# Two convolutional attention layers on one core: who evicts q and k, where zeros are written, and the order and queues of the last units

## The chip, the core and the metric

The kernel runs on one core of one Trainium2 chip. The metric is the device time of one execution in microseconds; the runs before the change have a median of 3063.85 us (three runs, 3060.79 to 3065.46). A core has five engines that run their own instruction queues and meet at semaphores: TensorE (PE in the profile) multiplies matrices into PSUM, VectorE (DVE) and ScalarE (ACT) work on SBUF and PSUM, GpSimd (POOL) and SyncE (SP) here mostly start DMAs. Sixteen DMA engines move data between DRAM and SBUF, whichever engine started the transfer.

## The reference

Two layers act on x, two images of 256 channels and 64 x 64 pixels, all in fp32. Layer 0 is attention over all 4096 pixels with 8 heads of 32 channels, mixed with x by a mask that is enlarged from 32 x 32:

```
q, k, v = conv1x1(x, Wq, bq)/sqrt(32), conv1x1(x, Wk, bk), conv1x1(x, Wv, bv)
fuse = softmax(q k^T) v                       # per head, 4096 x 4096
hybrid = conv1x1(concat(x, fuse), Wf, bf)
x = hybrid * m + x * (1 - m)
```

Layer 1 gates the channels, attends inside windows of 8 x 8 pixels, shuffles the channels and ends with two grouped 7 x 7 convolutions that give a gate:

```
x = x * sigmoid(relu(x @ ca_w1 + ca_b1) @ ca_w2 + ca_b2)
x = x + out_proj(window_attention(x))          # 4 heads of 64, windows of 64 tokens
x = channel_shuffle(x)
y = relu(bn1(conv7x7(x, sa_w1, groups=64)))
y = bn2(conv7x7(y, sa_w2, groups=64))
out = x * sigmoid(y)
```

## The kernel before

The order of the work on each engine is written out by hand; the framework adds only the waits. There are three parts.

**First part (L369 to L512).** x is cut into 16 chunks of 512 pixels (8 per image). For each chunk TensorE makes q and then k for 256 channels, 8 matmuls each (L432), into pairs of PSUM banks, of which three rotate. For each half `g` of the channels VectorE adds the bias and writes the result to SBUF (L442), and ScalarE squares the same PSUM half with the same bias into `sq` (L443). SyncE stores q (L447) and k (L450) to DRAM, and loads the chunk three ahead (L403). VectorE takes the largest sums of squares (L451), and one chunk later TensorE sums them by head (`norms`, L412): the product of the largest norms of q and k says whether the softmax can do without subtracting its maximum. The staging tiles of q, k and `sq` have two buffers each. After the 16 chunks TensorE makes v, 16 matmuls a chunk (L469); ScalarE copies it (L477) and GpSimd stores it (L482).

Beside this a generator `prepare` makes the constants, one step per chunk: GpSimd fetches weights and mask, VectorE folds the batch norms into the convolution weights. Its end writes zeros into the DRAM tensor `w_s` (16 units of 128 x 1792 floats, 896 KB each), from a zero tile in SBUF, by 16 DMAs of GpSimd (L327).

**Attention (L517 to L1182).** The 1024 `slots` are (image, chunk of 512 queries, half of the heads, block of 128 keys). In a slot TensorE makes the scores of four heads (L630), ScalarE their exponentials (L640), TensorE multiplies with v (L659) and VectorE adds the exponentials up (L661). k and v come in pieces of four slots, loaded two pieces ahead by SyncE into three buffers (L557, L559). Before the first slot SyncE issues, in this order, q, two pieces, the x chunk (L570) and the mask (L573); the third piece follows. After both halves of a chunk of queries, `stage` does the rest of layer 0 and the window attention in small steps between the slots (L718 to L979), and writes the rows to `x_s` in DRAM, on GpSimd (L976).

Between the slots another generator, `bands`, turns the convolution weights into band matrices: 156 DMAs of GpSimd within DRAM, which write strided elements into `w_s` over the zeros (L347, L353, L360). Every sixth slot takes one step of it (L1179). The steps stand in GpSimd's queue in that order, between the stores of the stages' rows, but a step waits for no slot.

**Last part.** `convolve` (L989) works through `items`, pairs of a unit (four groups of channels) and the images done together: units 0 to 6 of image 0, then units 1 to 6 of image 1, units 7 to 15 of both, at last unit 0 of image 1. For each item TensorE does the first convolution (L1040, from the rows loaded at L1019), ScalarE the relu (L1048), TensorE the second (L1064), ScalarE the tanh and a scaling (L1074, L1080), VectorE the product with x (L1086), and DMAs store the result, 12 per image, in turn by GpSimd and SyncE (L1096), for the last item by ScalarE and SyncE. The product tile z has two buffers. Weights of a unit come by SyncE (`load_w`, L1012) into the eight buffers that held exponentials, unit 0 into one of its own; unit u+8 is loaded when image 1's item of unit u is done.

The items are interleaved with the last stage, that of image 1's last rows: the stage gives `yield True` at six points (after L751, L791, L870, L877, L918, L945), and at each of them one step of `convolve` goes in. A step is either the second convolution of item k, or its product and stores and the first convolution of item k+2. Image 0 only is known then; rows with image 1 can be loaded once the stage has stored the last of them (`staged`). Loads of items 7 to 10 are then issued at once by `more()`, ahead of the next item's stores on SyncE.

```
items = [(u, (0,)) for u in range(EARLY)] + [(u, (1,)) for u in range(1, EARLY)]
items += [(u, (0, 1)) for u in range(EARLY, NU)] + [(0, (1,))]
```

Of the kernel before, what the change touches and what calls it, by code (L numbers as in the profile page):

```python
# [10 lines left out]
F32 = mybir.dt.float32  # L11
I32 = mybir.dt.int32
AF = mybir.ActivationFunctionType
# [4 lines left out]
B, C, H, W = 2, 256, 64, 64  # L18
N = H * W
P = 128  # L20
KC = C // P
# [9 lines left out]
EB = 8  # L31
DN = 8
EARLY = 7
# [13 lines left out]
NU = NG // UG  # L47
UW = UG * KS
# [7 lines left out]
def conv_seq_kernel(ctx: ExitStack, tc: tile.TileContext, a, out):  # L56
    nc = tc.nc
    const = ctx.enter_context(tc.tile_pool(name="const", bufs=1))
    dram = ctx.enter_context(tc.tile_pool(name="dram", bufs=1, space=bass.MemoryType.DRAM))
# [66 lines left out]
    w_s = dram.tile([NU, P, 2 * 32 * UW], F32, name="ws")  # L126
# [29 lines left out]
    for h in range(2):  # L156
        pending.append((cb1[64 * h : 64 * h + 64], a["ca_b1"]))
        pending.append((cw2[64 * h : 64 * h + 64], a["ca_w2"]))

    r1_s = dram.tile([32 + 4, NU, UW], F32, name="r1s")  # L160
    r2_s = dram.tile([32 + 4, NU, 4, UW // 4], F32, name="r2s")

# [2 lines left out]
    def prepare(mk, cwp):  # L165
# [55 lines left out]
        zero = cwp.tile([P, 2 * 32 * UW], F32, name="zero")  # L221
# [50 lines left out]
        for name, t in (  # L272
# [4 lines left out]
            g, beta, mean, var, cbias = (t[:, :, i] for i in range(5))  # L277
# [28 lines left out]
        for i in range(4):  # L306
            h, k = i % 2, i // 2
# [15 lines left out]
        nc.gpsimd.dma_start(  # L323
            r2_s.rearrange("p u i f -> p (u i f)"), m2.rearrange("p u i q x -> p (u i q x)")
        )
        for u in range(NU):
            nc.gpsimd.dma_start(w_s[u], zero)  # L327
            if u % 4 == 3:
                yield

# [5 lines left out]
    def bands():  # L338
        band1 = w_s.rearrange("u p (m f) -> u (p m) f", f=UW)
        band2 = w_s.rearrange("u p (m f) -> u (p m) f", f=UW // 4)  # L340
        for q in range(4):
            for dy in range(KS):
                r0, r1 = max(0, dy - PAD), min(RB, RB + dy - PAD)
                p0, m0, n = 32 * q + 1 + r0, 1 + r0 - dy + PAD, r1 - r0
                k = KS * q + dy
                at0, step = p0 * 64 + m0, 64 + 1
                nc.gpsimd.dma_start(  # L347
                    band1[:, at0 : at0 + step * (n - 1) + 1 : step, :], spread(r1_s[k : k + 1], n)
                )
                yield  # L350
                for i in range(4):
                    at0, step = p0 * 256 + 128 + i * 32 + m0, 256 + 1
                    nc.gpsimd.dma_start(  # L353
                        band2[:, at0 : at0 + step * (n - 1) + 1 : step, :],
                        spread(r2_s[k : k + 1, :, i], n),
                    )
                    yield
            for i in range(4):
                at0 = 32 * q * 256 + 128 + i * 32 + 1
                nc.gpsimd.dma_start(  # L360
                    band2[:, at0 : at0 + RB, :], spread(r2_s[32 + q : 33 + q, :, i], RB)
                )
                yield
# [5 lines left out]
    with (  # L369
# [8 lines left out]
        for n in ("WqT", "WkT", "WvT"):  # L378
            t = w0.tile([P, KC, C], F32, name=n)
# [3 lines left out]
        bias = {}  # L383
        for n in ("bq", "bk"):
            t = w0.tile([P, KC], F32, name=n)
# [33 lines left out]
        last = None  # L419
        for i, (b, c) in enumerate(chunks):  # L420
            load_chunk()
            x = xs0[i]
            sq = st0.tile([P, 2 * KC, CH], F32, tag="sq", name=f"sq_{b}_{c}")
            tops = st0.tile([P, 2 * KC, CH // 4], F32, tag="top4", name=f"top4_{b}_{c}")
            for n, w in (("q", wq), ("k", wk)):
                s = psum2(f"{n}0_{b}_{c}")
                for g in range(KC):
                    for kc in range(KC):
                        rhs = x[:, kc, :]
                        if n == "q":  # L430
                            rhs = rhs.rearrange("p (r w c) -> p w r c", r=WS, w=NW)
                        nc.tensor.matmul(  # L432
                            s[:, g, :],
                            w[:, kc, g * P : (g + 1) * P],
                            rhs,
                            start=(kc == 0),
                            stop=(kc == KC - 1),
                        )
                t = st0.tile([P, KC, CH], F32, tag=n, name=f"{n}st_{b}_{c}")
                bt = bias["b" + n]  # L440
                for g in range(KC):
                    nc.vector.tensor_scalar_add(t[:, g, :], s[:, g, :], bt[:, g : g + 1])  # L442
                    nc.scalar.activation(  # L443
                        sq[:, g + KC * (n == "k"), :], s[:, g, :], AF.Square, bias=bt[:, g : g + 1]
                    )
                if n == "q":
                    nc.sync.dma_start(q_s[b, c], t.rearrange("p g n -> p (g n)"))  # L447
                else:
                    for g in range(KC):
                        nc.sync.dma_start(k_s[b, g, c], t[:, g, :])  # L450
            nc.vector.tensor_reduce(  # L451
                tops, sq.rearrange("p g (n f) -> p g n f", f=4), AX.X, ALU.max
            )
            if i:
                norms(i - 1, last)
            last = tops
            for t, src in pending[4 * i : 4 * i + 4]:
                nc.scalar.dma_start(t, src)
            next(prepared, None)
# [61 lines left out]
    def pipeline(arm, shifted, pools):  # L521
# [196 lines left out]
        def stage(b, c):  # L718
# [173 lines left out]
                    )  # L892
            window_exp(1)
            nc.scalar.copy(v, sv)
            yield
            normalise(1)
            yield

# [83 lines left out]

        items = [(u, (0,)) for u in range(EARLY)] + [(u, (1,)) for u in range(1, EARLY)]
        items += [(u, (0, 1)) for u in range(EARLY, NU)] + [(0, (1,))]
        staged = []

        def convolve():  # L989
# [6 lines left out]
            for k in range(2):  # L996
                t = cpool.tile([P, B * nb, WP], F32, name=f"yc{arm}{k}")
                nc.gpsimd.memset(t, 0.0)
                ycs.append(t)
            xs, ws, ys = {}, {}, {}  # L1000
            dst = out.rearrange("b (g i) r w -> b i r g w", i=4)

            def load_w(u):
                if u >= NU:
                    return
                n = 2 * 32 * UW
                if u == 0:
                    t = cpool.tile([P, n], F32, name=f"w{arm}{u}")
                else:
                    t = ep.tile([P, HG, CH], F32, tag="e", name=f"w{arm}{u}")  # L1010
                    t = t.rearrange("p h n -> p (h n)")[:, 0:n]
                nc.sync.dma_start(t, w_s[u])  # L1012
                ws[u] = t
# [69 lines left out]
            def gate(k, z):  # L1083
                u, images = items[k]
                x = xs[k][:, 0 : nb * len(images), :, PAD : PAD + W]
                nc.vector.tensor_mul(z, z, x.rearrange("p n g x -> p g n x"))  # L1086

                last = k == len(items) - 1
                engines = (nc.scalar, nc.sync) if last else (nc.gpsimd, nc.sync)
                stores = 0  # L1090
                for m, b in enumerate(images):
                    for n, (x0, r0, r1) in enumerate(BLOCKS):
                        for i in range(4):
                            p = 32 * i + 1 - x0
                            stores += 1
                            engines[stores % len(engines)].dma_start(  # L1096
                                dst[b, i, r0:r1, UG * u : UG * u + UG, :],
                                z[p + r0 : p + r1, :, nb * m + n, :],
                            )
# [21 lines left out]
            for k, (u, images) in enumerate(items):  # L1121
                while len(xs) <= k + 1 < len(items):
                    if not more():
                        yield
                conv1(k + 1)
                yield
                more()
                z = conv2(k)
                yield
                more()  # L1130
                gate(k, z)
                if xcs or k + 4 < EARLY:
                    load_rows(k + 4)
                if B - 1 in images and u:
                    load_w(u + EB)

        def run_later():
            for _ in range(len(later)):
# [22 lines left out]
        for i, (b, c, g, m) in enumerate(slots):  # L1161
            now[0] = i
            if (b, c, g, m) == (B - 1, NCHUNK - 1, 0, 0):
                conv = convolve()
                next(conv)
            if m % PB == 0:
                load_piece(i // PB + AHEAD)
            if g == KC - 1 and m == 0:
                nxt = (b, c + 1) if c + 1 < NCHUNK else (b + 1, 0)
                if nxt[0] < B:  # L1170
                    load_q(*nxt)
            rest = scores(i + 2) if i + 2 < len(slots) else None
            products(i)
            if rest:
                rest()
            if g == KC - 1 and m == NMB - 1:
                at(DN + 5, lambda b=b, c=c: stages.append(stage(b, c)))
            run_later()
            if i % 6 == 1:  # L1179
                next(banded, None)  # L1180
            if i % 4 == 0:
                run_stages()  # L1182
# [102 lines left out]
```

## Time and profile before

The profiled execution took 3056.05 us; its span, from the first to the last instruction, is 3054.1 us. The granted TensorE clock is 0.99 of full speed on the mean.

| part of the span | us | TensorE busy | VectorE busy | ScalarE busy | DMA share |
|---|---|---|---|---|---|
| first part, to the first scores | 0 to 218.1 | 189.7 | 96.0 | 63.0 | 0.69 |
| attention | 218.1 to 2816.0 | 2574.6 | 2399.4 | 2303.6 | 0.31 |
| last part | 2816.0 to 3054.1 | 209.2 | 47.7 | 82.5 | 0.51 |

Busy times are sums of an engine's instructions; the DMA share is the mean busy share of the sixteen DMA engines. A busy TensorE is not TensorE at its peak, as matmuls overlap and their ends are modelled. In a row of the timeline, the bracket at the end says how long the engine was idle before the instruction, and what it then waited for. That releaser is inferred from semaphores: the last one to come by the profile.

In the first part VectorE spends 64 x 0.75 us at L442 and 16 x 2.29 us at L451, ScalarE 64 x 0.69 us at L443. The sixteen stores of zeros are issued from 103.1 to 129.4 us and take 23.2 us each (median) to land. In the last part a one-image item takes TensorE 2.5 us for the first and 3.6 us for the second convolution, a two-image item 4.8 and 5.0 us. A store of the result takes GpSimd 0.57 us of its queue.

### The profile page before, as it was taken

What the parts mean: (1) busy time and instruction counts of PE and PEld (TensorE: products, weight loads), DVE (VectorE), ACT (ScalarE), POOL (GpSimd) and SP (SyncE); (2) the same over time, 40 slices, a digit from 0 to 9 for tenths busy, and PEclk for the clock granted to TensorE, in tenths of its full rate; (3) what the DMA queues carried; (4) which work ended last, traced back from release to release, by engine and by line L of the source; (5) the groups of instructions that cost most, each with busy time, mean ns of one, the idle gap of its engine ahead of it and who ended that gap; (6) DMA issues with size and microseconds to landing.
All of it is one profiled execution on the core that took longest, in us unless ns stands there. A gap on an engine that the chain in (4) does not pass through costs nothing.

```text
span 3054.1 us, 60829 instructions
## 1 busy us (share of the span) xinstructions
PE 2973.5 (97%) x25114; PEld 1007.6 (33%) x25114; DVE 2543.1 (83%) x1411; ACT 2449.0 (80%) x4115; POOL 358.5 (12%) x617
## 2 busy tenths in 40 slices
PE   8899989999999999999999999999999999999997
PEld 3372222232322222222222222222222222233675
DVE  5519989999999999898999998999999998999111
ACT  2239979898989899898989898989898998988333
POOL 8130000001010101010100001010101010000256
PEclk9999999999999999999999999999999999999998
DMA  7854212324242424242322324232424242413364
GB/s 214 322 176 79 63 51 63 68 60 73 62 77 60 67 73 73 66 67 74 62 72 60 66 60 73 60 74 60 75 65 70 67 70 71 105 57 106 99 196 106
DMA packets 158703, 264.19 MB, mean 87 GB/s; under 512 B 44424, under 2 KB 63068, under 8 KB 158416
## 3 DMA queue, kind: packets, MB, share of 16 engines
q1 hardware_dynamic: 129056, 213.33, 25.3%
q0 software_dynamic: 24800, 44.16, 9.3%
q8 instruction: 200, 3.28, 0.5%
q10 hardware_dynamic: 4560, 2.70, 0.3%
q14 instruction: 87, 0.71, 0.1%
HBM read 197.89 MB, written 65.21 MB: 86 GB/s over the span
## 4 chain that ended last, share of the span: by engine, by line
PE 82%; DVE 6%; ACT 2%; DMA 2%; POOL 1%; issue 0%; SPq 0%; DVEq 0%
PE sa L630 34%; PE ava L659 31%; DVE suma L661 5%; PE qka L800 4%; PE hya L729 4%; PE c2a L1064 2%; PE vwa L886 2%; PE opa L950 2%; PE c1a L1040 1%; ACT ea L640 1%; POOL out_dram L1096 1%; PE sca L834 1%; PE rda L697 1%; PE ca2a L772 1%; PE pta L909 1%; PE oa L928 1%
## 5 line engine op out<-in xcount | busy, mean ns | idle before, releaser
L661 DVE TENSOR_TENSOR suma<-suma,ea 128x2048 f32<-128x2048 f32 x960 | 2198.5, 2290 | 86.8 <-ACT ea L640 3.9
L640 ACT ACTIVATE ea<-sa 128x512 f32<-128x512 f32 (+1 forms) x3072 | 2043.9, 745 | 85.6 <-PE sa L630 40.2
L630 PE MATMUL sa<-qa,ka 32*128 32x512 f32 x8192 | 1185.7, 640 | 4.8 <-DMA ka<-ks 3.4
L659 PE MATMUL ava<-ea,va 128*32 128x512 f32 x8192 | 1092.5, 605 | 0.3 <-ACT fa L669 0.3
L630 PEld LDWEIGHTS sa<-qa,ka 32*128 32x128 f32 x8192 | 330.2, 183 | 758.2 <-ACT ea L640 687.6
L659 PEld LDWEIGHTS ava<-ea,va 128*32 128x32 f32 x8192 | 161.6, 108 | 780.8 <-issue 753.8
L976 POOL DMA_DIRECT2D xs<-xo x94 | 65.9, 708 | 2334.3 <-DVE xo L961 2333.4
L800 PE MATMUL qka<-ua,qkv_w 128*128 128x512 f32 x256 | 118.4, 605 | 0.0
L1096 POOL DMA_DIRECT2D out_dram<-za x186 | 104.6, 570 | 106.0 <-DVE za L1086 62.8
L661 DVE TENSOR_TENSOR suma<-ea,ea 128x2048 f32<-128x2048 f32 x32 | 73.1, 2284 | 51.3 <-DMA ws<-r2s 51.3
L1086 DVE TENSOR_TENSOR za<-za,xla 128x1536 f32<-128x1536 f32 (+1 forms) x16 | 22.5, 1409 | 108.1 <-ACT za L1080 70.8
L1064 PE MATMUL c2a<-yca,wa 32*128 32x192 f32 (+1 forms) x1288 | 97.6, 444 | 4.1 <-ACT za L1074 3.6
L737 ACT ACTIVATE ta<-hya,bf 128x512 f32<-128x512 f32 x32 | 20.2, 684 | 96.8 <-PE hya L729 96.8
L1074 ACT ACTIVATE za<-c2a 128x384 f32<-128x384 f32 (+1 forms) x46 | 25.9, 614 | 87.5 <-DMA out_dram<-za 59.5
L1064 PEld LDWEIGHTS c2a<-yca,wa 32*128 32x128 f32 x1288 | 88.7, 314 | 14.7 <-issue 9.9
L741 DVE TENSOR_TENSOR ta<-ta,mca 128x512 f32<-128x512 f32 x32 | 22.0, 688 | 83.2 <-ACT ta L737 83.2
L855 ACT ACTIVATE ewa<-ewa,mxwa 128x64 f32<-128x64 f32 x256 | 85.5, 362 | 1.5 <-DVE mxwa L846 1.5
L443 ACT ACTIVATE sq<-q,bq 128x512 f32<-128x512 f32 x32 | 22.0, 687 | 76.5 <-DVE qst L442 73.2
L353 POOL DMA_DIRECT2D ws<-r2s x112 | 69.5, 623 | 76.8 <-DMA xs<-xo 42.8
L813 ACT ACTIVATE qka<-qka,qkv_b 128x512 f32<-128x512 f32 x64 | 40.7, 694 | 41.6 <-PE qka L800 41.6
L432 PE MATMUL q<-x,WqT 128*128 128x512 f32 x128 | 64.1, 647 | 5.7 <-DMA WqT<-in_WqT_dram 5.7
L800 PEld LDWEIGHTS qka<-ua,qkv_w 128*128 128x128 f32 x256 | 46.0, 189 | 71.3 <-issue 58.7
(140 smaller groups left out, 1655.9 us busy)
## 6 DMA issues: line engine op xcount, KB each, us to landing
ka<-ks SPq DMA_DIRECT2D x256, 256.0 KB
va<-vs SPq DMA_DIRECT2D x256, 256.0 KB
ws<-zero POOLq DMA_DIRECT2D x16, 896.0 KB, 23.2
wa<-ws SPq DMA_DIRECT2D x16, 896.0 KB
xs<-xo POOLq DMA_DIRECT2D x78, 140.0 KB, 7.8
xla<-xs SPq DMA_DIRECT2D x25, 420.0 KB
x<-in_x_dram SPq DMA_DIRECT2D x16, 512.0 KB
qs<-qst SPq DMA_DIRECT2D x16, 512.0 KB
```

The lines of the kernel that those rows point to most:

```text
L353: nc.gpsimd.dma_start(band2[:, at0 : at0 + step * (n - 1) + 1 : step, :], spread(r2_s[k : k + 1, :, i], n),)
L432: nc.tensor.matmul(s[:, g, :], w[:, kc, g * P : (g + 1) * P], rhs, start=(kc == 0), stop=(kc == KC - 1),)
L630: nc.tensor.matmul(heads[j], k[r, cols], q[r, g, :], start=True, stop=not shifted)
L640: nc.scalar.activation(e[:, h, :], tile, AF.Exp, scale=SCALE0)
L659: nc.tensor.matmul(av[r, :], v[:, m % PB, r], e[:, j, :], start=start, stop=stop)
L661: nc.vector.tensor_add(total, first[0] if m == 1 else total, e)
L729: nc.tensor.matmul(s[:, oc, :], wf[:, kc, oc * P : (oc + 1) * P], f[:, kc - KC, :] if half else xw[kc], start=(kc == 0), stop=(kc == 2 * K ...
L800: nc.tensor.matmul(s[:, j, :], wqkv[:, kc, o : o + P], u[:, kc, :], start=(kc == 0), stop=(kc == KC - 1),)
L855: nc.scalar.activation(e[:, n, :], e[:, n, :], AF.Exp, bias=mx[:, n : n + 1], accum_out=rs[:, n : n + 1],)
L976: eng.dma_start(x_s[b, n, p + r0 : p + r1].rearrange("r g w -> g r w"), xo[64 * h : 64 * h + 64, oc, r0 - WS * c : r1 - WS * c, :],)
L1064: nc.tensor.matmul(tiles[j // 2][:, j % 2, 0 : n * W], w[r, d], y[r, 0:n, d : d + W], start=(d == 0), stop=(d == KS - 1),)
L1096: engines[stores % len(engines)].dma_start(dst[b, i, r0:r1, UG * u : UG * u + UG, :], z[p + r0 : p + r1, :, nb * m + n, :],)
```

## The change

It touches three places.

In the first part ScalarE alone reads the PSUM tiles of q and k: it adds the bias by an Identity activation, half by half, and then squares the finished SBUF tile of both halves in one activation. VectorE's addition goes.

The zero tile is stored once, to a new DRAM tensor `zero_s`. `bands` begins with 16 steps that each copy `zero_s` to one unit of `w_s`, DRAM to DRAM, on GpSimd. Its steps are taken every fifth slot instead of every sixth, and what is left is issued before `convolve` starts (172 steps at every fifth slot end by slot 860, so nothing is left at slot 960).

In the last part the stage gets a seventh `yield True`, after the v matmuls of the windows. Unit 1 of image 1 moves from the eighth item to the last but one, so that the items end with two of one image; its weights are loaded a second time, and the order of the weight loads follows from a list. Once `staged` is set, items below 7 store on GpSimd only.

```diff
@@ prepare @@
-        for u in range(NU):
-            nc.gpsimd.dma_start(w_s[u], zero)
-            if u % 4 == 3:
-                yield
+        nc.gpsimd.dma_start(zero_s, zero)
+        yield
@@ bands @@
+        for u in range(NU):
+            nc.gpsimd.dma_start(w_s[u], zero_s)
+            yield
         for q in range(4):
@@ first part @@
                 for g in range(KC):
-                    nc.vector.tensor_scalar_add(t[:, g, :], s[:, g, :], bt[:, g : g + 1])
                     nc.scalar.activation(
-                        sq[:, g + KC * (n == "k"), :], s[:, g, :], AF.Square, bias=bt[:, g : g + 1]
-                    )
+                        t[:, g, :], s[:, g, :], AF.Identity, bias=bt[:, g : g + 1]
+                    )
+                nc.scalar.activation(sq[:, 0:KC] if n == "q" else sq[:, KC:], t, AF.Square)
@@ stage @@
             nc.scalar.copy(v, sv)
-            yield
+            yield True
             normalise(1)
@@ items, convolve @@
-        items = [(u, (0,)) for u in range(EARLY)] + [(u, (1,)) for u in range(1, EARLY)]
-        items += [(u, (0, 1)) for u in range(EARLY, NU)] + [(0, (1,))]
+        items = [(u, (0,)) for u in range(EARLY)] + [(u, (1,)) for u in range(2, EARLY)]
+        items += [(u, (0, 1)) for u in range(EARLY, NU)] + [(1, (1,)), (0, (1,))]
...
+            again = deque([*range(1 + EB, NU), 1])
...
-                last = k == len(items) - 1
-                engines = (nc.scalar, nc.sync) if last else (nc.gpsimd, nc.sync)
+                engines = (nc.gpsimd, nc.sync)
+                if k == len(items) - 1:
+                    engines = (nc.scalar, nc.sync)
+                elif staged and k < EARLY:
+                    engines = (nc.gpsimd,)
...
-                if B - 1 in images and u:
-                    load_w(u + EB)
+                if (u >= 2) == (B - 1 in images) and u and again:
+                    load_w(again.popleft())
@@ slots @@
             if (b, c, g, m) == (B - 1, NCHUNK - 1, 0, 0):
+                for _ in banded:
+                    pass
                 conv = convolve()
...
-            if i % 6 == 1:
+            if i % 5 == 1:
                 next(banded, None)
```

## The prediction

> **What bounds the kernel now.** I read the slices of the page first, then the groups by line, then the timeline of three stretches: the first part (0 to 218 us), the start of the attention (218 to 250) and the last part (2816 to 3054). The middle needs little: TensorE is busy 97% of the span, and the attention slots follow each other every 2.07 us plus the stages' own matmuls. Only what TensorE waits for in the three stretches can change.
>
> First part: a row of the page's groups (busy us, mean ns of one, idle before and its releaser), then the timeline (start, duration, engine, line, operation, idle before it and its releaser):
>
> ```profile
> L443 ACT ACTIVATE sq<-q,bq 128x512 f32<-128x512 f32 x32 | 22.0, 687 | 76.5 <-DVE qst L442 73.2
> ```
>
> ```profile
> 110.38 3.70 PE L432 MATMUL q<-x,WqT 128*128 128x512 f32 x8
> ...
> 118.00 3.70 PE L432 MATMUL q<-x,WqT 128*128 128x512 f32 x8
> ...
> 128.99 0.75 DVE L442 TENSOR_SCALAR qst<-q,bq 128x512 f32<-128x512 f32 x1 [3.56 <-DMA qs<-qst]
> 135.59 0.75 DVE L442 TENSOR_SCALAR kst<-k,bk 128x512 f32<-128x512 f32 x1 [4.28 <-DMA ks<-kst]
> 141.62 6.36 PE L432 MATMUL q<-x,WqT 128*128 128x512 f32 x8
> ...
> 150.00 0.75 DVE L442 TENSOR_SCALAR kst<-k,bk 128x512 f32<-128x512 f32 x1 [3.44 <-DMA ks<-kst]
> 156.03 5.99 PE L469 MATMUL v<-WvT,x 128*128 128x256 f32 x16
> ```
>
> See two things. VectorE and ScalarE evict the same PSUM tile in turns, each waiting for the other. A chunk then takes 7.62 us at best (110.38 to 118.00), which is also TensorE's own work (3.64 + 3.62 + 0.36 for the norms), but 8.57 us where preparation is added on VectorE (93.23 to 101.80). And from 125 to 156, while the sixteen 896 KB stores of zeros drain, VectorE waits for its own q and k stores and two chunks take some 15 us each.
>
> Windows of that stretch (busy time by engine, granted clock, DMA share, GB/s):
>
> ```profile
> 113.00:123.00 10.00, 9.87 (x31) 4.27 (x30) 6.19 (x8) 4.11 (x7) 1.74 (x4) 1.00 1.03 400
> 133.00:143.00 10.00, 6.45 (x17) 2.61 (x16) 3.98 (x4) 1.37 (x2) 0.00 (x0) 0.69 1.02 412
> ```
>
> All sixteen DMA engines are full. From 135.59 to 150.00 SyncE's queue moved one x chunk, one q and one k store, 1.57 MB in 14.4 us: 109 GB/s of about 412. The zeros had the rest.
>
> Start of the attention, and the last part:
>
> ```profile
> 221.88 0.38 SPq L570 DMA_DIRECT2D xa<-in_x_dram  x1
> ...
> 237.69 1.14 PE L630 MATMUL sa<-qa,ka 32*128 32x512 f32 x8 [3.36 <-DMA ka<-ks]
> ...
> 2869.51 0.69 PE L909 MATMUL pta<-ident,ewa 64*64 64x64 f32 x32 [1.95 <-DVE ewa L867]
> 2894.64 7.48 SPq L1096 DMA_DIRECT2D out_dram<-za  x12
> 2896.13 2.54 PE L1040 MATMUL c1a<-xla,wa 128*32 128x192 f32 x56 [1.68 <-DMA xla<-xs]
> 2901.95 0.87 ACT L1074 ACTIVATE za<-c2a 128x384 f32<-128x384 f32 x2 [10.51 <-DMA out_dram<-za]
> 2902.49 4.87 PE L1064 MATMUL c2a<-yca,wa 32*128 32x192 f32 x52 [3.11 <-ACT za L1074]
> 3037.66 0.87 ACT L1074 ACTIVATE za<-c2a 128x384 f32<-128x384 f32 x2 [4.18 <-DMA out_dram<-za]
> ```
>
> The attention starts with two pieces of k and v loaded. The third stands on SyncE behind the x chunk and the mask, which wait until 221.88: 1.05 MB before slot 8, landed 15.8 us later beside the band DMAs. Slots 8 to 10 lose 5.0 us to it (slot 10 starts at 243.41, where 2.07 us a slot from slot 7 at 232.20 gives 238.4). In the last part SyncE's stores stand behind loads that wait for the last rows, so a z buffer comes free late.
>
> **What the Trainium skill says.** "DMA: Bandwidth & Descriptors", section "Queues, rings and completion order": each DMA engine goes round robin between the queues that have work, one whole packet at a time, whoever issued. The 109 GB/s beside the zeros agree with small packets taking turns with 7 KB rows. Section "Why a DMA increments its semaphore by 16 and not by 1": one descriptor moves one contiguous run, up to 64 KiB, and a flat contiguous transfer is cut into a multiple of 16 pieces. No flat DRAM to DRAM copy is in this trace. Section "Latency and other measured facts" gives 214 GB/s for copies between HBM tensors in 16 KiB rows; the trace shows none. "ScalarE: Activation LUTs", section "Table sets": identity is in every set; the trace agrees, with three table loads in all although Exp, Identity, Tanh and Copy alternate.
>
> **The change, part by part.**
>
> *Eviction by ScalarE.* VectorE loses 64 x 0.75 us. ScalarE has, per chunk, 4 Identity of 128x512 from PSUM at 0.69 (L737's row, 684 ns) and 2 Squares of 128x1024 from SBUF, which no row shows; the nearest, the 128x1024 copies, took 1.01. That is 4.8 us, in the first four chunks also up to 4 DMA issues of 0.5: below 7.62. VectorE keeps its reduction (2.29) and small work. Of q and k each step stays ahead of TensorE, since three PSUM pairs rotate; the norms of a chunk need the reduction 4.9 us after its k matmuls, and come 7.3 us after them. So a chunk costs TensorE's 7.62. The start stays: the bias loads let ScalarE begin at 14.95 as now, third chunk at 23.6 (now 23.42). Then 14 x 7.62 gives 130.3 for the first v matmul, against 156.03: 25.7 us. Of it 15.1 are the zeros having left (118.00 + 3 x 7.62 would be 140.9), 10.6 the eviction. The v part now takes 60.9 (156.03 to 216.90), 16 x 3.45 plus a cold clock at first (16 matmuls in 5.99) and waits for the last norms; without the cold start 57.9, 3.0 less. Together -28.7, attention from 189.4 instead of 218.1. Bounds -32 and -15, the latter if ScalarE, in order, still holds the chunks at 8.57.
>
> *The zeros.* One SBUF store to the new tensor (0.9 MB, about 3 us of DMA near 103 us) remains and hides under the slack there. The sixteen copies are written among the slots, but GpSimd has nothing to wait for between them: now, too, it ran 21 band steps from 219.8 to 243 in one go and then idled 289 us for the first rows. It will issue all sixteen from about 191 (0.53 us each), and bands follow once they have landed. So 14.7 MB of copies fall just where the third k piece must arrive by 205.6 (234.3, where it is first missed, less 28.7).
>
> How much of the DMA the loads get depends on the packet. Source and target are both contiguous DRAM, 917,504 bytes; nothing keeps the rows apart as the SBUF partition did. I take the flat cut: 16 pieces of 57,344 bytes a copy, one per engine. Each engine then has 16 such packets, and between two of them one 2 KB packet of SyncE. Until the copies end the loads get 16 of the 32 packets per engine that the 1.05 MB need. A packet's price: at least 57,344 x 16 / 412 GB/s, 2.2 us; at most 4.3 us by the skill's 214 GB/s. I take 3.2, the middle. The third piece lands at 192 + 16 x (3.2 + 0.09) + 3 = 247.6, so slot 8 stands still 42 us. The old 5.0 us go. Bands, nine steps now behind the copies, meet loads that have fallen behind: I add 4 us for that and the clock after the pause. Net +41; from +25 to +59.
>
> Later only 13 band steps instead of 11 follow each stage's rows; such a burst at 534 us held nobody. They end by slot 860, before the first w load.
>
> *The last part.* The new True runs the next convolution step after the v matmuls: it fills the 1.95 us before L909's second half and keeps the clock, as the c1 after it took 4.15 instead of 2.54. Output matmuls end 0.95 us earlier with one c1 more behind them. Image 1's rows still need 13.6 us from there (2882.5 to 2896.1), now covered by 9.5 us of convolution, so TensorE waits 4 us there; but image 0's stores no longer stand behind the loads on SyncE, and the 3.1 us wait and the slow c2 go. By my account c2 of the eighth unit ends 5.1 us earlier. GpSimd's 12 stores cost 6.73 us a unit against 5.98 of TensorE; over three units that lags 2.3 us, which two z buffers hide. Two small units last: the last z waits for the 24 stores two units back, about 1.5 us longer than now, while SyncE has 6 fewer stores after it: -0.4. One more w load (0.9 MB) lands long before its use. Sum -5.5, bounds -9 and +3.
>
> *Sum.* The profiled execution took 3056.05 us (span 3054.1 and 1.95 around it). 3056.05 - 28.7 + 41 - 5.5 = 3062.9, +6.8. The median of the runs lies 7.8 above the profiled one: 3063.85 + 6.8, about 3071.
>
> **Rivals.**
>
> *Packets stay rows of 7 KB* (the tile's own shape kept). Then loads and copies alternate 2 KB with 7 KB as in the first part; at 214 to 400 GB/s the loads get 53 to 100 GB/s where the attention needs 63 (512 KB in 8.27 us). The third piece is 0 to 9 us late, later ones at most 9 more in all. With the old 5.0 gone and 3 for bands: +3 instead of +41, 3063.85 - 31 = 3033, from 3026 to 3046. For it: the pattern is written as 128 rows. Against it: nothing needs them. It decides below some 28 KB a packet, where all 32 load packets find turns before the copies end. This case is not slower.
>
> *ScalarE becomes the bound of the first part*: 8.57 a chunk stays, 13 us of the saving are missing, 3084 with large packets. For it: its queue also issues weights and two square roots. Against: 4.8 of 7.62 us.
>
> *The copies at 2.2 us a packet*: still large packets, but the stall is 16 x 2.29 + 195 - 205.6 = 26 us, total 3055; no change at 2.8 us; 3088 at 4.3.
>
> **How the numbers follow.** Large packets 0.60 (faster 0.13, within 0.14, slower 0.33, as the packet's price may fall), rows 0.28 (all faster), ScalarE or a worse last part 0.12 (slower). A measurement tells about 0.2%, 6 us, from no change. Faster 0.41, within 0.14, slower 0.45. Own range of the likeliest: 3055 to 3088; the whole range 3029 to 3090.
>
> **What would show it.** First v matmul near 130 and chunks of 7.6 us: eviction right; 143, ScalarE binds. L630 after slot 7 with a wait of 20 to 60 us for ka<-ks: large packets; under 10, rows. L909 without its 1.95 and c1 on xla waiting about 4 us: last part right. I am wrong if copies don't start together near 191.

## The result and the profile after

In twelve runs of each, the changed kernel took 3061.73 us (median; 3058.31 to 3075.2) and the kernel before 3063.19 (3055.48 to 3068.36). The ratio is 1.0003, with a 95% interval of 0.9993 to 1.0014: no difference that can be measured. (Here and below the ratio is not the quotient of the two medians, which is 0.9995 here and lies inside the interval.) The profiled execution after took 3062.01 us with a span of 3060.2, that of before 3056.05 and 3054.1; the 6.1 us between the spans can be placed from the marks of the two timelines:

| stretch | before | after | difference |
|---|---|---|---|
| span's start to the attention's first scores | 218.09 | 187.13 | -30.96 |
| first scores to the first convolution matmul (c1a) | 2600.54 | 2638.94 | +38.40 |
| first convolution matmul to the span's end | 235.45 | 234.15 | -1.30 |

The two marks of before:

```profile
218.09 3.06 PE L630 MATMUL sa<-qa,ka 32*128 32x512 f32 x16 [1.19 <-ACT vst L477]
...
2818.63 2.88 PE L1040 MATMUL c1a<-xea,wa 128*32 128x192 f32 x56
```

So nothing was small here. One stretch won 31 us, the next one lost 38, and the two nearly cancel.

The first part, in the timeline of after (start, duration, engine, line, operation, idle before it and its releaser):

```profile
105.28 3.70 PE L434 MATMUL q<-x,WqT 128*128 128x512 f32 x8
108.82 3.60 PE L434 MATMUL k<-x,WkT 128*128 128x512 f32 x8
112.35 0.43 PE L414 MATMUL nrm<-top,headsum 128*32 128x128 f32 x8
112.70 3.70 PE L434 MATMUL q<-x,WqT 128*128 128x512 f32 x8
...
127.54 3.72 PE L471 MATMUL v<-WvT,x 128*128 128x256 f32 x16
...
187.13 3.06 PE L632 MATMUL sa<-qa,ka 32*128 32x512 f32 x16 [1.19 <-ACT vst L479]
```

A chunk takes 7.42 us and TensorE has no gap in it; before it took 8.57 where VectorE also prepared. ScalarE's rows by form (busy us, mean ns of one, idle before and its releasers) show that it isn't the bound:

```profile
L444 ACT ACTIVATE kst<-k,bk 128x512 f32<-128x512 f32 x32 | 20.2, 681 | 11.3 <-PE k L434 11.3
L447 ACT ACTIVATE sq<-kst 128x1024 f32<-128x1024 f32 x16 | 16.9, 1056 | 0.5
```

Four Identities of 0.68 and two Squares of 1.06 are 4.84 us a chunk, and before each pair ScalarE waits for the matmuls, not they for it.

The attention's start, timeline of after; `SPq` and `POOL` lines are DMA issues:

```profile
189.56 3.40 POOL L341 DMA_DIRECT2D ws<-zeros  x7 [0.19 <-issue]
191.08 0.38 SPq L572 DMA_DIRECT2D xa<-in_x_dram  x1
191.59 0.41 SPq L575 DMA_DIRECT2D mca<-masks  x1
192.12 0.43 SPq L559 DMA_DIRECT2D ka<-ks  x1
...
216.09 0.49 POOL L341 DMA_DIRECT2D ws<-zeros  x1 [2.87 <-DMA ws<-zeros]
241.08 2.09 PE L632 MATMUL sa<-qa,ka 32*128 32x512 f32 x8 [37.69 <-DMA ka<-ks]
241.22 0.65 POOL L349 DMA_DIRECT2D ws<-r1s  x1 [24.64 <-DMA ws<-zeros]
```

GpSimd waits for no slot: it issues eight copies from 188.84 to 192.96 and each of the other eight as soon as an earlier copy has landed, the last at 216.09, so that copies are always queued. The third piece of k, issued at 192.12, is there only at 241.08, 0.14 us before GpSimd finds its last copy landed. TensorE stands still for 37.69 us. Windows of after around it (us, then busy us and instructions of PE, PEld, DVE, ACT and POOL; granted clock; DMA share; GB/s):

```profile
190.00:203.00 13.00, 12.74 (x97) 3.10 (x96) 10.13 (x5) 12.74 (x21) 4.42 (x10) 1.00 1.09 361
203.00:241.00 38.00, 0.39 (x4) 0.00 (x0) 5.91 (x3) 1.41 (x3) 2.44 (x5) 0.54 0.96 311
241.00:280.00 39.00, 38.92 (x280) 8.82 (x280) 31.94 (x14) 33.80 (x51) 5.56 (x9) 0.92 0.39 68
```

TensorE is busy 0.39 of 38 us while the DMA engines are full.

The last part, timeline of after:

```profile
2826.07 2.88 PE L1043 MATMUL c1a<-xea,wa 128*32 128x192 f32 x56
...
2833.75 2.65 PE L1067 MATMUL c2a<-yca,wa 32*128 32x192 f32 x40
2840.19 1.68 PE L1067 MATMUL c2a<-yca,wa 32*128 32x192 f32 x16 [3.79 <-issue]
2841.65 2.02 PE L699 MATMUL rda<-inva,spread_h 32*128 32x128 f32 x16
2843.60 6.02 PE L731 MATMUL hya<-xa,WfT 128*128 128x512 f32 x8
...
2883.09 1.16 PE L911 MATMUL pta<-ident,ewa 64*64 64x64 f32 x64
2884.18 3.58 PE L1067 MATMUL c2a<-yca,wa 32*128 32x192 f32 x56
...
2908.44 4.72 PE L1043 MATMUL c1a<-xla,wa 128*32 128x192 f32 x56 [4.04 <-DMA xla<-xs]
2913.09 3.58 PE L1067 MATMUL c2a<-yca,wa 32*128 32x192 f32 x56
```

Both halves of L911 run as one group of 64, the wait of 3.11 us for za is gone and one of 4.04 for xla has come, as forecast. New is the top: a gap of 3.79 us inside the first c2 group, with no releaser named, and a first hya of 6.02 us, in which the granted clock was 0.61 of full speed. Before had here

```profile
2829.70 1.02 PE L1064 MATMUL c2a<-yca,wa 32*128 32x192 f32 x12 [0.51 <-issue]
2832.17 3.70 PE L729 MATMUL hya<-xa,WfT 128*128 128x512 f32 x8
```

### The profile page after: what moved, and what is told of

Its sections match the earlier page's. It is cut to its first block, busy times and chain, and to the rows that moved or that the text cites. A ratio compares the mean times of both kernels' runs of the same rounds, so it can differ in the third digit from the quotient of the medians.

```text
span 3060.2 us, 60785 instructions
## 1 busy us (share of the span) xinstructions
PE 2967.3 (97%) x25114; PEld 1005.6 (33%) x25114; DVE 2498.5 (82%) x1347; ACT 2478.7 (81%) x4147; POOL 369.4 (12%) x636
## 4 chain that ended last, share of the span: by engine, by line
PE 71%; DVE 13%; DMA 4%; issue 2%; ACT 2%; POOL 1%; SPq 0%; DVEq 0%; ACTq 0%
PE sa L632 29%; PE ava L661 27%; DVE suma L663 11%; PE qka L802 4%; PE hya L731 4%; DMA ka<-ks 2%; PE vwa L888 2%; ACT ea L642 1%; PE opa L952 1%; PE c2a L1067 1%; POOL out_dram L1102 1%; DMA wa<-ws 1%; PE c1a L1043 1%; PE sca L836 1%; PE rda L699 1%
## 5 line engine op out<-in xcount | busy, mean ns | idle before, releaser
L1102 POOL DMA_DIRECT2D out_dram<-za x204 | 114.9, 571 | 102.4 <-DVE za L1089 55.5
L453 DVE TENSOR_REDUCE top<-sq 128x512 f32<-128x2048 f32 x16 | 36.6, 2286 | 81.4 <-ACT sq L447 81.4
```

The source lines that it names most:

```text
L1102: engines[stores % len(engines)].dma_start(dst[b, i, r0:r1, UG * u : UG * u + UG, :], z[p + r0 : p + r1, :, nb * m + n, :],)
```

## The experiments

Theory: three changes that add up; the gain of the first part is real, and the copies, issued as fast as GpSimd can and in packets of 57,344 bytes, leave the loads of k and v one small packet for each large one. Rivals: the mere volume of the copies does it; the attention, starting earlier, runs out of loaded pieces whatever the copies do; something of the gain was never there.

### Each part alone

Eviction alone, on the kernel before:

```
+   nc.scalar.activation(t[:, g, :], s[:, g, :], AF.Identity, bias=bt[:, g : g + 1])
+ nc.scalar.activation(sq[:, 0:KC] if n == "q" else sq[:, KC:], t, AF.Square)
```

> The kernel before with the eviction by ScalarE alone; zeros and last part as before. If VectorE and ScalarE in turns cost 10.6 us of the first part (my step), the first v matmul comes near 145 instead of 156 and the kernel is 10 to 14 us faster, about 3050. If in that stretch the stores of q and k, slow beside the zeros, are what holds the chunks whoever evicts, the first v comes after 150 and the gain is under 6 us.

3043.9 us, ratio 0.9940 (0.9926 to 0.9953). The first v matmul, timeline of this run:

```profile
137.91 5.22 PE L469 MATMUL v<-WvT,x 128*128 128x256 f32 x16
```

That is earlier than either side expected, 18.1 us before the old 156.03, and the time is below the 3050 us expected. By the start of the thirteenth chunk (110.38 before, 97.77 here) 12.6 us are won, and 5.5 more in the last four chunks, though there ScalarE now waits for the stores of q and k (up to 6.38 us).

Zeros alone, on the kernel before (with the steps of `bands` at every fifth slot, as in the change):

```
+ zero_s = dram.tile([P, 2 * 32 * UW], F32, name="zeros")
- for u in range(NU): nc.gpsimd.dma_start(w_s[u], zero)       # in prepare
+ nc.gpsimd.dma_start(zero_s, zero)
+ for u in range(NU): nc.gpsimd.dma_start(w_s[u], zero_s)     # in bands
```

> The kernel before with the zeros alone moved among the slots as copies in DRAM. My account: -15 in the first part (two chunks no longer wait for stores), +38 for the third piece of k, -5 for the old loss at slots 8 to 10: about +18, 3081. The loads start 15 us earlier but the copies start with them, so the wait at slot 8 (L630) is again 35 to 42 us. If the change's standstill came from the attention starting earlier (pieces of k and v loaded less far ahead) rather than from the copies, the wait is under 20 us and the time at or below 3063.

3083.0 us, ratio 1.0068 (1.0054 to 1.0082). Timeline of this run:

```profile
141.09 3.72 PE L471 MATMUL v<-WvT,x 128*128 128x256 f32 x16
...
258.73 2.09 PE L632 MATMUL sa<-qa,ka 32*128 32x512 f32 x8 [37.41 <-DMA ka<-ks]
```

The wait is the same, 37.41 against 37.69 us, though the attention starts at 205.06 here and at 187.13 there. With the eviction alone, which starts the attention at 199.33 without any copies there, the wait at slot 8 is 4.67. So it comes with the copies, not with an early start. This doesn't yet tell packets from volume.

Last part alone, on the kernel before:

```
- yield
+ yield True
...
- items = [(u, (0,)) for u in range(EARLY)] + [(u, (1,)) for u in range(1, EARLY)]
- items += [(u, (0, 1)) for u in range(EARLY, NU)] + [(0, (1,))]
+ items = [(u, (0,)) for u in range(EARLY)] + [(u, (1,)) for u in range(2, EARLY)]
+ items += [(u, (0, 1)) for u in range(EARLY, NU)] + [(1, (1,)), (0, (1,))]
...
+ elif staged and k < EARLY:
+     engines = (nc.gpsimd,)
...
- if B - 1 in images and u:
-     load_w(u + EB)
+ if (u >= 2) == (B - 1 in images) and u and again:
+     load_w(again.popleft())
```

> The kernel before with the last part's edits alone (the yield that goes on to convolution, image 0's stores on GpSimd, two one-image units last, w of unit 1 loaded again). My step: -5.5 (-9 to +3), 3057.5. Rival: the 6.3 us that c2a (3.79 with no releaser named) and hya lost at the start of the convolution in the profile of the changed kernel come with these edits, then the sum is near 0, 3063, and the same two rows show it here.

3059.94 us, ratio 0.9995 (0.9983 to 1.0007); a gap of 2.63 us in the first c2 group, hya 6.02. This fits the rival, but the zeros alone, without these edits, have 3.75 and 5.87 there. So these edits are not needed for the gap. The three ratios multiplied give 1.0003, that of the whole change: within their intervals of some 0.1% each the parts add.

### The size of a packet

Same bytes, same place, another cut:

```
- nc.gpsimd.dma_start(w_s[u], zero_s)
+ nc.gpsimd.dma_start(w_s[u], zero_s, max_dma_last_dim=7168)   # 14336, 28672
```

> The changed kernel, but each copy of zeros is cut into 128 pieces of 7,168 bytes instead of 16 of 57,344; the same 14.7 MB at the same place. If the size of the packets starves SyncE's loads, the score matmuls of slot 8 (L632) wait under 10 us for ka<-ks instead of 37.7, and the kernel takes about 3063 - 30 = 3033 us (3026 to 3046). If the volume of the copies beside the loads is what counts, 30 us or more of the wait stay and the time is within 6 us of the changed kernel's 3062.

> The changed kernel, copies cut into packets of 14,336 bytes. Turn-taking: each engine then has 64 packets of copies, SyncE's loads need 32 turns ahead of the third piece, so they are through after half the copies, 32 x (0.73 + 0.09) = 26 us after 193; the wait at slot 8 is 13 to 20 us (10.2 at 7 KB, 37.7 at 56 KB), the time 3036 to 3041. If instead any copy beyond the 7 KB row size loses the loads their place altogether (a threshold), the wait is 33 us or more and the time near 3058.

> The changed kernel, copies cut into packets of 28,672 bytes. Turn-taking: 32 packets of copies on each engine, as many as the loads need turns, so the third piece lands only as the copies end: halving the packet gains almost nothing, wait at slot 8 of 33 to 38 us, time 3056 to 3062. If the wait follows the packet's size in proportion, it is about 20 us and the time 3043.

| packet, bytes | wait at slot 8, us | time, us | ratio to before (95%) |
|---|---|---|---|
| 7,168 | 10.2 | 3030.6 | 0.9895 (0.9878 to 0.9911) |
| 14,336 | 17.6 | 3042.5 | 0.9940 (0.9923 to 0.9956) |
| 28,672 | 29.9 | 3055.3 | 0.9973 (0.9963 to 0.9983) |
| 57,344 (the change) | 37.7 | 3061.7 | 1.0003 (0.9993 to 1.0014) |

Volume is out: the same 14.7 MB cost 31 us less in packets of 7 KB. Nor did the pace of the issues change: at 7 KB too GpSimd issued eight copies by 193.25 and the last at 221.94, as others landed. That the cut is what it was taken for is in the page's queue rows (packets, MB, share of 16 engines), first of after, then of the 7 KB run:

```profile
q0 software_dynamic: 23728, 45.48, 9.8%
```

```profile
q0 software_dynamic: 25520, 45.48, 9.8%
```

1,792 more packets are 16 copies x (128 - 16). The wait of the 7 KB run is just over the 10 us that were named, the time of the 14 KB run 1.5 us above its range, and the 28 KB run fell between its two expectations. Counting the packet records of GpSimd's queue (q0) and SyncE's (q1) in the trace, all 16 engines together, while the third piece is held up says why:

```
kernel   window, us         q0 data      q0 of 4 B   q1 of 2,048 B and 4 B
57,344   195.75 to 233.75   204          204         378 + 28
28,672   195.75 to 225.75   312          160         438 + 32
14,336   195.75 to 215.75   382          100         438 + 33
 7,168   195.75 to 208.75   445           62         471 + 31
```

Both queues sent nearly the same number of packets, 408 and 406, 472 and 470, 482 and 471, 507 and 502. The Trainium skill says in "DMA: Bandwidth & Descriptors", section "Queues, rings and completion order", that an engine takes the queues in turn, a packet at a time. The counts agree with turns, but not with the skill's size of a packet, typically 9 to 17 descriptors: here one record of the trace went for one of the other queue. (The kept trace doesn't name a packet's engine, so it shows equal counts, not the single turns.) And a copy ends on each engine with a 4-byte packet, which I take for its semaphore write; the counts are equal only if that takes a turn as well. A copy thus grants the loads two turns an engine at 57,344 bytes, three at 28,672, five at 14,336, nine at 7,168; I had counted one, two, four and eight. A 57,344-byte packet took 2.73 us here on average.

### Where the copies stand

Copies on SyncE, at the same slots of the program:

```
- nc.gpsimd.dma_start(w_s[u], zero_s)
+ nc.sync.dma_start(w_s[u], zero_s)
```

> The changed kernel with the sixteen copies issued by SyncE instead of GpSimd, at the same slots of the program (1, 6, 11 ...), in their large packets. SyncE's order puts the third piece of k and v ahead of the first copy and its loads wait for free buffers, so that one copy of some 3 us falls between loads and the copies can't start together; the bands on GpSimd need all sixteen and move away from the start, too. If it is the sixteen copies queued at once that starve the loads, the wait at slot 8 (L632, 37.7) falls under 6 us and the time is 3062 - 38 to - 43 = 3019 to 3024, below the 3030.6 of the small packets. If large packets hurt the loads wherever they stand, each copy costs its 3 us: 16 x 3 = 48 us, and the time stays near 3060.

3024.1 us, ratio 0.9879 (0.9864 to 0.9894). Timeline of this run, then its window:

```profile
192.21 0.35 SPq L559 DMA_DIRECT2D ka<-ks  x1
192.61 0.42 SPq L561 DMA_DIRECT2D va<-vs  x1
193.09 0.58 SPq L341 DMA_DIRECT2D ws<-zeros  x1
...
199.98 0.48 SPq L341 DMA_DIRECT2D ws<-zeros  x1
...
203.61 1.14 PE L632 MATMUL sa<-qa,ka 32*128 32x512 f32 x8
...
208.29 0.47 SPq L341 DMA_DIRECT2D ws<-zeros  x1
```

```profile
203.00:241.00 38.00, 38.00 (x300) 8.65 (x296) 36.34 (x17) 36.82 (x56) 0.00 (x0) 1.00 0.41 137
```

Slot 8 starts at 203.61 without a wait, and TensorE is busy all of the 38 us in which it was busy 0.39. The packets are as large as ever; one copy at a time holds up no slot here. But two things changed: pace and queue. (The bands, which wait for all sixteen copies, moved as well; in the changed kernel they begin only at 241.22, after the wait.) Two runs part them, ScalarE issuing at the same slots, and SyncE issuing all sixteen at slot 1 (the `yield` after each copy moved behind the loop).

> The changed kernel with the copies issued by ScalarE at slots 1, 6, 11 ... in large packets: another queue than the loads', so the packets still take turns with the loads', but ScalarE reaches each copy only when the evictions of the slots ahead of it are done. If it is the pacing that helped with SyncE, slot 8 waits under 6 us again and the time is 3024 plus at most 16 x 0.5 us of ScalarE's issues, 3022 to 3032. If it was that copies and loads share one queue and so stand in order, the copies in a queue of their own stop the loads again: wait over 10 us, time over 3035.

> The changed kernel with all sixteen copies issued by SyncE back to back at slot 1, behind the third piece of k and v and ahead of the fourth. Pacing: slot 8 has its piece, but the fourth stands behind 14.7 MB in the same queue, 16 x 2.9 = 46 us, lands near 242 where slot 12 needs it at 212: a wait of some 30 us moves to slot 12, time 3050 to 3060. Shared queue: if standing in order with the loads is enough, no wait over 10 us and a time under 3035.

ScalarE: 3023.5 us, ratio 0.9866 (0.9831 to 0.9901), no wait at slot 8, one copy about every 10.3 us (194.62, 204.95, 215.28). The burst on SyncE: 3049.9 us, ratio 0.9957 (0.9946 to 0.9968), and its timeline

```profile
192.81 27.13 SPq L341 DMA_DIRECT2D ws<-zeros  x16
...
209.53 1.14 PE L632 MATMUL sa<-qa,ka 32*128 32x512 f32 x8
222.37 0.34 SPq L559 DMA_DIRECT2D ka<-ks  x1
...
244.10 2.09 PE L632 MATMUL sa<-qa,ka 32*128 32x512 f32 x8 [32.42 <-DMA ka<-ks]
```

shows the wait moved on to slot 12, whose piece stands behind the copies in the same queue. It is the pace, on whichever queue. SyncE and ScalarE have a pace because they wait for what TensorE frees; GpSimd waits only for its own earlier copies there.

### The last part beside an undisturbed start

The run with copies on SyncE, its last part set back to that of before:

> As the run with copies on SyncE, but with the last part of the kernel before. Its distance to that run is the last part's worth beside an undisturbed start: my step says 5.5 us slower than that run, the run with the last part's edits alone (0.9995 of before) says 1 to 2 us slower or nothing that can be measured.

3027.41 us, ratio 0.9881 (0.9864 to 0.9897) against 0.9879: the medians differ by 3.3 us, the intervals overlap. To see more I cut the end of all timelines at the end of the v matmuls (L888 in after):

| run | first c1 to end of v matmuls | from there to span's end |
|---|---|---|
| before | 48.3 | 187.2 |
| zeros alone | 54.2 | 183.9 |
| SyncE, old last part | 53.3 | 182.0 |
| after | 54.6 | 179.5 |
| last part alone | 53.8 | 180.9 |
| SyncE, new last part | 53.1 | 178.9 |

These are single profiled executions. The right column has the edits' gain; the left one has the gap. The instruction packets in the trace point to its source: TensorE went on at 2829.70 in before and at 2840.19 in after, and 16,384-byte packets of the instruction queue had come in at 2828.42 and 2838.72. In all twelve traces with the gap, these two among them, TensorE went on 1.3 to 1.6 us after the end of such a packet. Just then eight w loads of 896 KB, issued back to back (2814.21 to 2832.28 in after), hold the DMA engines (share 0.94 from 2814 to 2833). So I spread them, three at the start and one per unit after that:

```
- for u in range(1, 1 + EB): load_w(u)
+ for u in range(1, 4): load_w(u)
  for k, (u, images) in enumerate(items):
+     if 0 < k <= EB - 3: load_w(k + 3)
```

> The run with copies on SyncE, and of the eight w loads (896 KB each) that the convolution issues back to back at its start only three there, the other five one per unit, from the second unit on. In all runs TensorE stops inside the first c2 group (0.5 to 3.8 us with no releaser named) and goes on about 1.1 us after a 16,384-byte instruction packet has come in, while these loads fill the DMA engines; the projection hya then runs at a slow clock. If the instructions stand behind the w loads, the gap falls under 1 us, hya back to 3.7 us and the time to 3024 - 4 to - 5, about 3019. If the gap has another cause, it stays at 2 to 4 us and the time at 3024.

> The kernel before with the last part's edits alone, and the w loads spread in the same way. The run without the spread gave 0.9995 of before: its records after the attention win 5 us or more, but the first c2 group and hya lose 5.5. If the w loads cause that loss, this one is 5 to 7 us faster than before, ratio near 0.998; if not, it stays near 0.9995.

The last part alone with this spread: 3054.87 us, ratio 0.9972 (0.9962 to 0.9983), against 0.9995 (0.9983 to 1.0007) without. On top of the SyncE copies: 3020.26 us, ratio 0.9854 (0.9831 to 0.9878), the fastest median of all, though its interval overlaps that of the run without the spread. Timeline of the latter run:

```profile
2801.18 3.58 PE L1067 MATMUL c2a<-yca,wa 32*128 32x192 f32 x56
2804.58 1.47 PE L699 MATMUL rda<-inva,spread_h 32*128 32x128 f32 x16
2805.97 3.70 PE L731 MATMUL hya<-xa,WfT 128*128 128x512 f32 x8
```

The c2 group is whole, hya is back to 3.70, and the left column of the table would be 47.25 us in both runs. The instruction packet starts 5.4 us after the first c1, where it started 8.6 us after it in before and 11.6 in after.

## Why the prediction was right, and where not

The verdict was not the likeliest forecast: 3071 us was said, 3061.7 measured, within the range, and no difference where slower had the larger chance. The mechanism held in the main; its sizes and its last addition did not. That the sum for the profiled execution came within 1 us is luck: the three parts missed by -2.3, -2.6 and +4.2 us, which nearly cancel.

*The first part.* Forecast -28.7, measured -30.96. The first v matmul came at 127.54 instead of the forecast 130.3, since a chunk of TensorE's own work is 7.42 us, not 7.62 (the 7.62 of before held small pauses). The split between the two causes was off: I gave 10.6 us to the eviction and 15.1 to the zeros having left. Alone, up to the first scores, they gave 18.8 (218.09 to 199.33) and 13.0 (218.09 to 205.06). The rival that ScalarE becomes the bound fell with 4.84 us of 7.42.

*The zeros.* Forecast +41 net, measured +38.40; wait 42 us forecast, 37.69 measured, at the slot named. The copies didn't all start together near 191: eight did, and the others followed one by one until 216.09, each behind a landed one. For the loads it came to the same, since copies were queued without a break. They were cut into sixteen pieces each (256 packets of 57,344 bytes), as the section "Why a DMA increments its semaphore by 16 and not by 1" of the same page led me to expect; the rival of 7 KB rows fell, and when I made it true it came to 3030.6, against the 3033 worked out for it. The term that was mis-sized is the price of a packet: 3.2 us taken, 2.73 measured, 336 GB/s over sixteen engines. The page's 214 GB/s for copies in 16 KiB rows (section "Latency and other measured facts"), which made the upper bound of 4.3, was far from it for these flat copies. The other error hid itself: with one turn a copy, the loads would have been half through when the copies ended. The other half would have followed within some 3 us by my sum. With two, they need 32 / 2 = 16 copies, all of them, so the piece arrives about when the copies end either way.

*The last part.* Forecast -5.5, measured -1.30. From the end of the v matmuls on the forecast is right: the fifth c2 group from there starts 38.4 us later in after (2880.68 to 2919.06) and 43.3 in before (2866.94 to 2910.24), 4.9 us gained where I said 5.1; over the runs without a spread, the right column has a mean of 179.4 with the new last part (eight runs, 177.2 to 180.9) and 184.4 with the old one (four, 182.0 to 187.1), -5.0. What the forecast lacked stands ahead of that point: +6.3 us, of which the gap and the slow hya make 5.6. That instructions come over the same DMA engines, and can come late beside eight w loads, was in no step. Removing the burst removes it, so the w loads' part is shown; that the late packet is the link is not shown: it rests on its times alone. Why it is late by 0.5 us in before and by 3.8 in after stays open: zeros alone and last part alone each suffice.

*The sum.* My sum for a profiled execution was 3062.9, the profile after shows 3062.01. Then I added the 7.8 us by which the runs' median lay above the profiled execution of before, and this is the term that was wrong. The profile of after lies 0.3 us from its own median; over the twelve experiments the profiled execution lay between 3.9 us below and 7.6 above the median of its kernel. A single execution's distance from the median isn't a constant of the kernel that a change carries along. By the medians the change made the kernel 1.5 us faster, by the two profiles 6 us slower; only the interval, 0.9993 to 1.0014, says what can be said.

## What to carry to other kernels

Bulk copies that are moved off a crowded stretch need something that paces them. In this kernel it was enough to put them on an engine that waits for the critical engine's progress; look at what the issuing engine itself waits for, not at where the line stands in the program. If they can't be paced, cut them smaller: at 7,168 bytes a packet the wait was 10.2 us, at 57,344 it was 37.7. And when a large edit measures as nothing, run its parts alone: here they were worth -0.60%, +0.68% and -0.05% (the last within the noise), and moving the issue of the sixteen copies to another engine turned 3062 into 3024 us.

## What the runs showed of the hardware that I had not expected

- The 4-byte packet at the end of a copy seems to take a turn between queues like any other: 408 against 406 packets at 57,344 bytes, 204 of the 408 with 4 bytes, and nearly equal counts at three other sizes.
- Beside such copies SyncE's queue moved 20 GB/s in all (378 packets of 2,048 bytes in 38 us) while the copies moved 308.
- TensorE stood up to 3.79 us in the middle of a group of equal matmuls, with no releaser in the trace, and went on 1.3 to 1.6 us after a 16,384-byte instruction packet had come in; the next projection then took up to 6.02 us instead of 3.70, at a granted clock of 0.61 in the changed kernel. Spreading five of eight 896 KB loads removed both.
